# Batch 0's product from a ready-made diagonal, four turns handed to another path, and the last mix and store split by chunk

## The chip, the cores and the metric

The kernel runs on one core of a Trainium2 chip. The metric is the device time of one execution in microseconds; before the change it is 1623.7 us, the median of three executions (1623.25 to 1623.99). The profile is of one execution, with a span of 1622.2 us from its first to its last instruction.

The engines are named as in the profile: PE multiplies matrices and writes to banks of PSUM (the kernel has eight of them); PEld loads PE's weights and overlaps it; DVE and ACT work element by element; POOL does small jobs (here the power -1/2); SP issues transfers (DMA). All data here is float32, and a float32 matmul appears in the profile as two instructions, called passes here. A PE transpose is one pass pair as well: four 128x128 blocks of one batch give four instructions.

## The reference, cut to what matters

32 batches of 512 nodes with 128 features go through four graph layers that share one 512x512 adjacency matrix, each with a layer norm before it and a residual after it.

```python
# x: (32, 512, 128), adj: (512, 512)
# layer 0: normalised adjacency
h = relu(layernorm(x))
A = adj + I;  d = A.sum(-1) ** -0.5
x = x + ((d[:, None] * A * d[None, :]) @ h) @ W.T + b
# layer 1: five gated steps
h = relu(layernorm(x))
for _ in range(5):
    m = adj @ h                                   # m_in == m_out
    av = concat([m, m])
    z = sigmoid(av @ w3.T + b3 + h @ u3.T + bu3)
    r = sigmoid(av @ w4.T + b4 + h @ u3.T + bu3)
    hv = tanh(av @ w5.T + b5 + (r * h) @ u5.T + bu5)
    h = (1 - z) * h + z * hv
x = x + h
# layers 2 and 3: graph attention (2 ends in elu, 3 doesn't)
for l in (2, 3):
    h = relu(layernorm(x)) @ W_l
    e = leaky_relu((h @ a_src) + (h @ a_dst).T, 0.2)
    p = softmax(where(edge, e, -inf))
    x = x + (elu if l == 2 else identity)(p @ h)
```

## The kernel before

The kernel first records every piece of work (`op`) with its engine, an assumed cost, a due number, and what it reads and writes. When all is recorded, a list scheduler plays the program through with the assumed costs: whenever an engine is free it takes, of the pieces that are ready and find their buffers free, the one with the smallest `soon`. The order so found is the order in which the instructions are written out, so a due number is a priority on an engine and not a time. The schedule is played for some pairs (last, hurry), six times each, and the one with the earliest end is kept. `near_end` (1350) says from where on, in the scheduler's own time, a piece is ordered by how late it may be.

```python
EARLY = 8
FAR0, FAR1 = 2, 4
# ... (the scheduler)
o.soon = min(o.due, last - o.tail * hurry)                               # first try
o.soon = late[o] / self.SLOT if o.at > self.near_end else o.due          # the next ones
# ... (the buffers, then:)
    }, [(179, 0.06), (175, 0.06), (177, 0.12)], 1350, IDLE_FROM, ...)
```

Layer 0 of batches 0 to 3 multiplies by the raw adjacency plus the unit matrix. `diag` holds the four diagonal blocks with 1 added; batches 1 to 3 use it, batch 0 adds a separate multiplication by the unit matrix.

```python
diag = Val("v", C)
for m in range(C):
    op("DVE", 0.16, -6, lambda m=m: nc.vector.tensor_add(diag.t[:, m, :], block(adjT.t, m), ident.t), ...)

def product(h, due, by_diag):                    # by_diag is False for batch 0 alone
    for c in range(C):
        row = adjT.t[:, c, :]
        if by_diag:
            terms = [(0, c, row[:, :c * P]), (c, c + 1, diag.t[:, c, :]), (c + 1, C, row[:, (c + 1) * P:])]
        else:
            terms = [(0, C, row), (c, c + 1, ident.t)]
        # ... one matmul for each term that isn't empty            (L671)
    op("ACT", A, due, lambda: nc.scalar.copy(flat(m.t), flat(p.t)), ...)
```

In layer 1 a state is needed in both orientations. At its start, and after each of the five steps, it is turned either by PE (four transposes into a bank, then a copy by ACT) or by a shuttle: DVE transposes 32x32 squares, four transfers write them to DRAM and another one or four read them back in place.

```python
def to_features(y, due, *then):                  # PE's turn: 4 transposes              (L560)
def shuttle(src, squares, dst, halves, due, soon):
    # DVE transpose of squares, two halves                                             (L570)
    # 4 DMAs sq -> far (DRAM)                                                          (L577)
    # 2 DMAs far -> dst, one for each half                                             (L581)

# in ggnn(pair, due), due = 5 * pair[0]
if FAR0 <= b < B - FAR1:
    shuttle_first(h, hT, due - 2.5, due - 3)
else:
    p = to_features(h, due - 2, hT)              # and one ACT copy

# in step(b, s, m, hT, due, lane), called with due = 5 * pair[0] + 6 * s + (0 or 1)
if not EARLY <= due < STEPS * B:                 # STEPS * B = 160
    p = to_features(new, due + 2, ...)           # and two ACT copies (L796), or an addition to x after the last step
    return h, new
if not last:
    shuttle(new, None, h, True, due, due - 5)
```

The last four batches do their attention "near": no shuttle, masks in SBUF. Four chunks c of 128 nodes are mixed into two banks, two chunks in each.

```python
ps, rden, v, n = (Val("bank"), Val("bank")), Val("rden", 2), Val("v", 2), Val("r", 2)
if near:
    for j in range(C):
        def mix_from(j=j):                       # 4 chunks, 8 passes                   (L903)
            for c in range(C):
                nc.tensor.matmul(<bank c // 2, place c % 2>, e.t[:, j, c * P:(c + 1) * P], h.t[:, j, :D + 1],
                                 start=j == 0 and c % 2 == 0, stop=j == C - 1, ...)
        op("PE", C * MM1, due + 4, mix_from, r=[e[j], h[j // 2], h[2 + j // 2]], w=[*ps])
for a, p in enumerate(ps):
    op("DVE", 0.08, due + 4, <reciprocal of two chunks' sums>, ...)                  # L917
    # layer 3: two scalar_tensor_tensor, one for each chunk                           (L925)
# layer 3, near: one store for each half of the nodes, 128 KB                         (L947)
```

Of the kernel before, what the change touches and what calls it, by code (L numbers as in the profile page):

```python
# [15 lines left out]
P = 128  # L16
# [5 lines left out]
NEAR = 4  # L22
EARLY = 8
FAR0, FAR1 = 2, 4
IDLE_FROM = 1420
# [230 lines left out]
def gnn_stack(ctx: ExitStack, tc: tile.TileContext, a: dict, out: bass.AP):  # L256
# [13 lines left out]
    def flat(t):  # L270
# [33 lines left out]
        "rden": tiles(3, SMALL, "rden"),  # L304
    }, [(179, 0.06), (175, 0.06), (177, 0.12)], 1350,
        IDLE_FROM, lambda v: nc.tensor.transpose(v.t[:, 0, :], ident.t, ident.t))
# [50 lines left out]

    op("DVE", 0.2, -15, lambda: nc.vector.tensor_scalar_add(b0.t, b0.t, -1.0), w=[b0])
    for k in ("w4", "w3", "w5", "u3", "u5"):
# [5 lines left out]
    for l, w in ((2, "L2_gnn_W"), (3, "L3_gnn_w")):  # L365
        w_aug[l] = fixed([P, D + 3], f"w_aug{l}", 2)
        op("SP", 0.45, -990.5, lambda l=l, w=w: nc.sync.dma_start(w_aug[l].t[:, :D], a[w]), w=[w_aug[l][0]], delay=3.4)
        a_pair[l] = fixed([P, 2], f"a_pair{l}", 2)
        for i, k in enumerate(("src", "dst")):
            op("SP", 0.45, -990.4, lambda l=l, i=i, k=k: nc.sync.dma_start(  # L370
                a_pair[l].t[:, i:i + 1], column(a[f"L{l}_gnn_a_{k}"])), w=[a_pair[l][i]], delay=2.4)
# [18 lines left out]
    def block(t, m):  # L390
        return t[:, m, m * P:(m + 1) * P]
# [3 lines left out]
    for m in range(C):  # L395
        op("DVE", 0.16, -6, lambda m=m: nc.vector.tensor_add(diag.t[:, m, :], block(adjT.t, m), ident.t),
           r=[adjT, ident], w=[diag[m]])

    def right_factors(mT, due, passing=False):
# [13 lines left out]
        return f  # L413
    of_adj = right_factors(adjT, -5)

# [36 lines left out]

    w0T = transposed(-9.2, (one(w0), 1), then=turned)
    gates = transposed((-700, -9.5, -700, -9.5), (halves("w4"), 1), (one(raw["u3"]), 1), (halves("w3") + halves("w4", minus), 1), (halves("w5"), 1), then=turned)
    u5T = transposed(-9.4, (one(raw["u5"]), 0.5), then=turned)
    gats = transposed(-4, (one(w_aug[2]), 1), (one(w_aug[3]), 1))
    gate_b = {}
# [8 lines left out]
    for i, l in enumerate((2, 3)):  # L466
        p = Val("bank")
        op("PE", 0.3, -3, lambda i=i, l=l, p=p: nc.tensor.matmul(p.t[:, 0, :2], gats.t[:, i, :], a_pair[l].t, start=True, stop=True),
           r=[gats, a_pair[l]], w=[p])

        def columns(l=l, p=p):
            for j, (s, f) in enumerate(((1, SLOPE), (1, 1.0 - SLOPE), (0, SLOPE - 1.0))):
                nc.vector.tensor_scalar_mul(w_aug[l].t[:, D + j:D + j + 1], p.t[:, 0, s:s + 1], f)
        op("DVE", 0.3, 10, columns, r=[p], w=[w_aug[l][1]])
# [183 lines left out]

    def product(h, due, by_diag):

        p, m = Val("bank"), Val("m")
        for c in range(C):
            def times(c=c):
                row = adjT.t[:, c, :]
                if by_diag:
                    terms = [(0, c, row[:, :c * P]), (c, c + 1, diag.t[:, c, :]), (c + 1, C, row[:, (c + 1) * P:])]
                else:
                    terms = [(0, C, row), (c, c + 1, ident.t)]
                terms = [t for t in terms if t[0] < t[1]]
                for k, (lo, hi, right) in enumerate(terms):  # L670
                    nc.tensor.matmul(flat(p.t)[:, lo * P:hi * P], h.t[:, c, :], right, start=c == k == 0,  # L671
                                     stop=c == C - 1, skip_group_check=True)
            op("PE", MM if by_diag else MM + 0.1, due, times, r=[h[c], adjT, diag[c] if by_diag else ident], w=[p, m])
        op("ACT", A, due, lambda: nc.scalar.copy(flat(m.t), flat(p.t)), r=[p], w=[m])
        return m

    def normalized(begun):
# [5 lines left out]
        def turn_dinv():  # L683
            for c in range(C):
                nc.tensor.transpose(drow.t[:, c, :], dinv.t[:, c:c + 1].to_broadcast([P, P]), ident.t)
        op("PE", C * TURN, -2, turn_dinv, r=[dinv, ident, begun], w=[drow])
        op("DVE", 0.1, -790, lambda: nc.vector.tensor_mul(dinv2.t, dinv.t, dinv.t), r=[dinv], w=[dinv2])

        for m in range(C):
            op("DVE", 0.7, -1, lambda m=m: nc.vector.scalar_tensor_tensor(  # L690
                anT.t[:, m, :], adjT.t[:, m, :], dinv.t[:, m:m + 1], flat(drow.t), op0=ALU.mult, op1=ALU.mult),
# [3 lines left out]
               r=[ident, dinv2], w=[anT[m]])  # L695
        return anT, right_factors(anT, 0, True)

# [3 lines left out]
    def gcn(pair, due):  # L701
        first, ys = pair[0] < 4, []
        for i, b in enumerate(pair):
# [3 lines left out]
            else:  # L707
                norm_relu(b, y, -797 if b == 1 else due + i, dinv if first else None)
            op("DVE", V, due + i + 1, lambda b=b: nc.vector.tensor_add(
                xs[b].t, xs[b].t, b0.t[:, None, :].to_broadcast([P, C, D])), r=[b0], w=[xs[b]])  # L710
            ys.append(y)

        ms = [product(y, due + i, pair[i] > 0) for i, y in enumerate(ys)] if first else products(*ys, factors["an"], due + 1)
        if b == 1:
            factors["anT"], factors["an"] = normalized(ms[0])
        for i, (b, m) in enumerate(zip(pair, ms)):
            p = Val("bank")

            def out_mm(m=m, p=p):
                for c in range(C):  # L720
                    nc.tensor.matmul(p.t[:, c, :], m.t[:, c, :], w0T.t[:, 0, :], start=True, stop=True)  # L721
            op("PE", C * MM1, due + i + 1.5, out_mm, r=[m, w0T], w=[p])
            if first:
                for c in range(C):
                    op("DVE", 0.26, due + i + 1.5, lambda b=b, c=c, p=p: nc.vector.scalar_tensor_tensor(
                        xs[b].t[:, c, :], p.t[:, c, :], dinv.t[:, c:c + 1], xs[b].t[:, c, :], op0=ALU.mult, op1=ALU.add),
                       r=[p, dinv], w=[xs[b][c]])
# [7 lines left out]
    def ggnn(pair, due):  # L735
        hs, hTs, lanes = [], [], []
        for b in pair:
            lane, h, hT = Val("lane"), Val("h", 2), Val("hT", Q)
            op("SP", 0.0, due - 3, lambda: None, r=[xs[b]], w=[lane], delay=0)
            op("SP", 0.0, due - 3, lambda: None, r=[lane], w=[h], delay=0)  # L740
            norm_relu(b, h, due - 3)
            if FAR0 <= b < B - FAR1:
# [67 lines left out]
    def masks(begun):  # L810

        maskT = {l: fixed([P, Q, N], f"maskT{l}", C, dtype=BF16) for l in (2, 3)}
        for l in (2, 3):
            far = Val(None, C)
            far.t = tiles(1, [Q, W, C, N], f"far_mask{l}", dram, BF16)[0]
            for c in range(C):
                part = Val("mask", 1)
                edges(l, c, part, lambda part=part: part.t, 14 + l, begun)
                op("SP", 0.4, 14 + l, lambda c=c, far=far, part=part: nc.sync.dma_start(
# [11 lines left out]
    def gat(b, l, due):  # L831
# [61 lines left out]
        for j in range(C):  # L893
            op("DVE", 0.68, due + 3, lambda j=j: nc.vector.scalar_tensor_tensor(  # L894
                e.t[:, j, :], rows(row.t), h.t[:, j, D + 1:D + 2], mask(j), op0=ALU.max, op1=ALU.mult),
               r=[row, h[2 + j // 2], masked], w=[e[j]])
        ps, rden, v, n = (Val("bank"), Val("bank")), Val("rden", 2), Val("v", 2), Val("r", 2)
        if near:

            for j in range(C):  # L900
                def mix_from(j=j):
                    for c in range(C):
                        nc.tensor.matmul(flat(ps[c // 2].t).rearrange("p (c k) -> p c k", c=2)[:, c % 2, :D + 1],  # L903
                                         e.t[:, j, c * P:(c + 1) * P], h.t[:, j, :D + 1], start=j == 0 and c % 2 == 0,
                                         stop=j == C - 1, skip_group_check=True)
                op("PE", C * MM1, due + 4, mix_from, r=[e[j], h[j // 2], h[2 + j // 2]], w=[*ps])
        for a, p in enumerate(ps):
            pt = lambda p=p: flat(p.t).rearrange("p (c k) -> p c k", c=2)
            some = slice(2 * a, 2 * a + 2)
            for c in range(2 if not near else 0):  # L910
# [5 lines left out]
                op("PE", C * MM1, due + 4, mix, r=[e, h], w=[*ps] if a == c == 0 else [p])  # L916
            op("DVE", 0.08, due + 4, lambda some=some, pt=pt: nc.vector.reciprocal(rden.t[:, some], pt()[:, :, D]), r=[p], w=[rden[a]])  # L917
            if l == 2:
                op("DVE", 0.335, due + 4, lambda some=some, pt=pt: nc.vector.tensor_mul(
                    v.t[:, some], pt()[:, :, :D], rden.t[:, some, None].to_broadcast([P, 2, D])), r=[p, rden[a]], w=[v[a]])  # L920
            else:
                def finish(a=a, pt=pt):
                    for c in range(2):
                        i = 2 * a + c
                        nc.vector.scalar_tensor_tensor(xb.t[:, i, :], pt()[:, c, :D], rden.t[:, i:i + 1], xb.t[:, i, :],  # L925
                                                       op0=ALU.mult, op1=ALU.add)
                op("DVE", 2 * 0.26, due + 4, finish, r=[p, rden[a]], w=[xb[2 * a], xb[2 * a + 1]])
        if l == 2 and near:
# [16 lines left out]
        elif near:  # L945
            for a in range(2):
                op("SP", 0.45, due + 4, lambda a=a: nc.sync.dma_start(  # L947
                    out[b].rearrange("(c p) d -> p c d", p=P)[:, 2 * a:2 * a + 2], xb.t[:, 2 * a:2 * a + 2]),
                   r=[xb[2 * a], xb[2 * a + 1]])
        else:  # L950
# [3 lines left out]
    def begin(b):  # L954
        gcn((b, b + 1), STEPS * b - (16 if b == 2 else 10))

# [58 lines left out]
```

## Time and profile before

| what | value |
|---|---|
| time, median of 3 | 1623.7 us (1623.25 to 1623.99) |
| span of the profiled execution | 1622.2 us |
| DVE busy | 1378.4 us (85% of the span) |
| ACT busy | 725.3 us (45%) |
| DMA queue of the kernel's transfers | 39.0% of 16 engines' span |
| PE's first instruction | 1.05 us after the start |
| PE's turns (L560): of new states, of first states, of the attention's input | 48, 24 and 32 instructions, four to a turn |

Busy time is the union of the durations that the profile gives. For PE those durations overlap: an instruction is shown from its start to a modelled end, while the next one starts earlier than that. What a group of PE's instructions takes from the next group is therefore read from the distance between starts, or from the chain of work, which merges neighbours and counts no time twice. The chain of work is followed back from the last instruction: at each step to whatever released it, or else to the instruction before it on the same engine.

### The profile page before, as it was taken

What the parts mean: (1) busy time and instruction counts of PE and PEld (TensorE: products, weight loads), DVE (VectorE), ACT (ScalarE), POOL (GpSimd) and SP (SyncE); (2) the same over time, 40 slices, a digit from 0 to 9 for tenths busy, and PEclk for the clock granted to TensorE, in tenths of its full rate; (3) what the DMA queues carried; (4) which work ended last, traced back from release to release, by engine and by line L of the source; (5) the groups of instructions that cost most, each with busy time, mean ns of one, the idle gap of its engine ahead of it and who ended that gap; (6) DMA issues with size and microseconds to landing.
All of it is one profiled execution on the core that took longest, in us unless ns stands there. A gap on an engine that the chain in (4) does not pass through costs nothing.

```text
span 1622.2 us, 24004 instructions
## 1 busy us (share of the span) xinstructions
PE 1614.2 (100%) x7326; PEld 1168.2 (72%) x7326; DVE 1378.4 (85%) x3971; ACT 725.3 (45%) x1628; POOL 146.4 (9%) x137
## 2 busy tenths in 40 slices
PE   9999999999999999999999999999999999999998
PEld 8666667776776777777777776777767686677778
DVE  8968588888888898888898888988888788888888
ACT  5644453535345353453544345343453524443554
POOL 2200000011001110001010011000010000000100
PEclk9999999999999999999999999999999999999999
DMA  4134243544535344353543535345353343334101
GB/s 131 27 78 117 66 115 87 131 100 102 124 79 138 92 105 115 90 132 78 129 106 92 137 79 123 99 100 128 85 128 87 85 99 78 104 97 112 40 22 52
DMA packets 374177, 157.72 MB, mean 97 GB/s; under 512 B 201664, under 2 KB 355616, under 8 KB 374048
## 3 DMA queue, kind: packets, MB, share of 16 engines
q1 hardware_dynamic: 373760, 155.67, 39.0%
q8 instruction: 58, 0.95, 0.2%
q14 instruction: 71, 0.58, 0.1%
q10 hardware_dynamic: 288, 0.52, 0.1%
HBM read 86.25 MB, written 69.84 MB: 96 GB/s over the span
## 4 chain that ended last, share of the span: by engine, by line
PE 94%; DVE 3%; DMA 1%; ACT 0%; POOL 0%; issue 0%; SPq 0%; DVEq 0%; ACTq 0%; POOLq 0%
PE bank L628 33%; PE bank L914 12%; PE bank L762 8%; PE bank L763 8%; PE bank L776 8%; PE bank L769 8%; PE bank L777 8%; PE bank L852 3%; PE bank L721 2%; PE bank L903 2%; PE bank L671 1%; PE bank L560 1%; DVE st L480 0%; POOL rstd L493 0%; DMA e<-in_adj_dram 0%
## 5 line engine op out<-in xcount | busy, mean ns | idle before, releaser
L493 POOL TENSOR_TENSOR rstd<-ve,mhalf 128x4 f32<-128x4 f32 x119 | 135.1, 1137 | 1382.2 <-DVE ve L485 1243.4
L628 PE MATMUL bank<-made,S 128*128 128x256 f32 x960 | 230.7, 380 | 0.5 <-DVE m L641 0.3
L914 PEld LDWEIGHTS bank<-h_gat,e 128*128 128x128 f32 x1792 | 210.6, 191 | 13.0 <-issue 10.5
L633 ACT COPY half<-bank 128x256 f32<-128x256 f32 x282 | 104.6, 371 | 243.6 <-PE bank L628 239.1
L914 PE MATMUL bank<-h_gat,e 128*128 128x129 f32 x1792 | 212.4, 275 | 0.0
L628 PEld LDWEIGHTS bank<-made,S 128*128 128x128 f32 x960 | 184.2, 196 | 31.3 <-issue 12.3
L765 ACT ACTIVATE r<-bank,gate_bw 128x512 f32<-128x512 f32 x160 | 109.6, 685 | 206.3 <-PE bank L763 188.9
L781 DVE TENSOR_TENSOR hv<-hv,hT 128x512 f32<-128x512 f32 x160 | 109.2, 683 | 81.7 <-ACT hv L779 81.5
L767 DVE SCALAR_TENSOR_TENSOR rh<-r,hT 128x512 f32<-128x512 f32 x160 | 109.7, 686 | 67.6 <-ACT r L765 65.8
L762 PE MATMUL bank<-m,wT 128*128 128x512 f32 x320 | 163.6, 593 | 0.1
L776 PE MATMUL bank<-m,wT 128*128 128x512 f32 x320 | 163.5, 592 | 0.0
L763 PE MATMUL bank<-hT,wT 128*128 128x512 f32 x320 | 163.4, 592 | 0.0
L777 PE MATMUL bank<-rh,wT 128*128 128x512 f32 x320 | 163.4, 592 | 0.0
L779 ACT ACTIVATE hv<-bank,gate_bw 128x512 f32<-128x512 f32 x160 | 109.7, 686 | 119.5 <-PE bank L777 119.4
L769 PE MATMUL bank<-m,wT 128*128 128x512 f32 x320 | 163.1, 592 | 0.0
L894 DVE SCALAR_TENSOR_TENSOR e<-row,h_gat,maskT 128x512 f32<-128x512 f32 x224 | 160.7, 741 | 0.0
L628 PE MATMUL bank<-adjT,h 128*128 128x256 f32 x640 | 159.7, 380 | 0.0
L628 PEld LDWEIGHTS bank<-adjT,h 128*128 128x128 f32 x640 | 123.0, 196 | 25.9 <-issue 14.4
L641 DVE TENSOR_TENSOR m<-half,bank 128x256 f32<-128x256 f32 x282 | 115.8, 413 | 26.9 <-PE bank L628 15.7
L771 ACT ACTIVATE z<-bank,gate_bw 128x512 f32<-128x512 f32 x160 | 109.5, 685 | 42.6 <-PE bank L769 39.9
L480 DVE BATCH_NORM_STATS2 st<-x 128x6 f32<-128x128 f32 x480 | 116.0, 279 | 7.0 <-DMA x<-in_x_dram 6.7
L763 PEld LDWEIGHTS bank<-hT,wT 128*128 128x128 f32 x320 | 60.8, 190 | 76.5 <-issue 76.1
(146 smaller groups left out, 2366.9 us busy)
## 6 DMA issues: line engine op xcount, KB each, us to landing
far<-sq SPq DMA_DIRECT2D x920, 64.0 KB
h<-far SPq DMA_DIRECT2D x240, 128.0 KB
gT<-far SPq DMA_DIRECT2D x56, 256.0 KB
row<-line SPq DMA_DIRECT2D x56, 256.0 KB
x<-in_x_dram SPq DMA_DIRECT2D x32, 256.0 KB
h<-far SPq DMA_DIRECT2D x28, 256.0 KB
out_dram<-x SPq DMA_DIRECT2D x28, 256.0 KB
hT<-far SPq DMA_DIRECT2D x104, 64.0 KB
```

The source lines that it names most:

```text
L480: op("DVE", 0.21, due, lambda c=c: nc.vector.bn_stats(st.t[:, c, :], xb.t[:, c, :]), r=[xb[c]], w=[st[c]])
L493: op("POOL", 1.0, due, lambda: nc.gpsimd.tensor_tensor(rstd.t, ve.t, mhalf.t, ALU.pow), r=[ve, mhalf], w=[rstd])
L628: nc.tensor.matmul(low(r), u[:, l, :], factors[k][0]()[:, l, :], start=fresh and l == 0, stop=l == 1, skip_group_check=not fresh)
L641: op("DVE", HV, due - 5, lambda: nc.vector.tensor_add(out(), u.t, low(t)), r=[u, t], w=[o])
L762: nc.tensor.matmul(flat(gate.t), gates.t[:, 0, :], flat(m.t), start=True, stop=False)
L763: nc.tensor.matmul(flat(gate.t), gates.t[:, 1, :], flat(hT.t), start=False, stop=True)
L767: op("DVE", V, due - 5, lambda: nc.vector.scalar_tensor_tensor(flat(rh.t), flat(r.t), 1.0, flat(hT.t), op0=ALU.add, op1=ALU.mult), r=[r, h ...
L769: op("PE", MM, due + 0.3, lambda: nc.tensor.matmul(flat(gate.t), gates.t[:, 2, :], flat(m.t), start=False, stop=True, skip_group_check=Tru ...
L776: nc.tensor.matmul(flat(cand.t), gates.t[:, 3, :], flat(m.t), start=True, stop=False)
L777: nc.tensor.matmul(flat(cand.t), u5T.t[:, 0, :], flat(rh.t), start=False, stop=True)
L894: op("DVE", 0.68, due + 3, lambda j=j: nc.vector.scalar_tensor_tensor(e.t[:, j, :], rows(row.t), h.t[:, j, D + 1:D + 2], mask(j), op0=ALU. ...
L914: nc.tensor.matmul(pt()[:, c, :D + 1], e.t[:, j, i * P:(i + 1) * P], h.t[:, j, :D + 1], start=(j == 0), stop=(j == C - 1))
```

## The change

It has five parts.

1. Batch 0 uses the diagonal tile as batches 1 to 3 do. The multiplication by the unit matrix goes; the four additions that make the tile come earlier in DVE's order.
2. `EARLY` goes from 8 to 6. The states of batches 0 and 1 after the second step (s = 1, due 6 and 7) are shuttled instead of turned by PE.
3. `FAR1` goes from 4 to 2. The first states of batches 28 and 29 are shuttled as well.
4. For batch 31's layer 3, the mix goes into four banks, one for each chunk. Its last two sources are taken chunk by chunk, and each chunk is divided, added and stored by itself (64 KB).
5. Many due numbers of the first slots and the scheduler's pairs of (last, hurry) and `near_end` are set anew.

```diff
-EARLY = 8
-FAR0, FAR1 = 2, 4
+EARLY = 6
+FAR0, FAR1 = 2, 2
-    }, [(179, 0.06), (175, 0.06), (177, 0.12)], 1350,
+    }, [(167, 0.1), (181, 0.05)], 1300,
-    op("DVE", 0.2, -15, ... b0.t, b0.t, -1.0 ...)
+    op("DVE", 0.2, -38.7, ...)
-        op("SP", 0.45, -990.5, ... w_aug ..., delay=3.4)
+        op("SP", 0.45, -990.5, ... w_aug ..., delay=5)
-        op("DVE", 0.16, -6, ... diag ...)
+        op("DVE", 0.26, -800 + 0.7 * m, ... diag ...)
-    of_adj = right_factors(adjT, -5)
+    of_adj = right_factors(adjT, -3.6)
-    w0T = transposed(-9.2, ...)
-    gates = transposed((-700, -9.5, -700, -9.5), ...)
-    u5T = transposed(-9.4, ...)
-    gats = transposed(-4, ...)
+    w0T = transposed(-11.7, ...)
+    gates = transposed((-700, -9.5, -700, -15.8), ...)
+    u5T = transposed(-15.2, ...)
+    gats = transposed(-0.4, ...)
-        op("PE", 0.3, -3, ... a_pair ...)
+        op("PE", 0.3, 9, ... a_pair ...)
-    def product(h, due, by_diag):
+    def product(h, due):
-                if by_diag:
-                    terms = [(0, c, row[:, :c * P]), (c, c + 1, diag.t[:, c, :]), (c + 1, C, row[:, (c + 1) * P:])]
-                else:
-                    terms = [(0, C, row), (c, c + 1, ident.t)]
+                terms = [(0, c, row[:, :c * P]), (c, c + 1, diag.t[:, c, :]), (c + 1, C, row[:, (c + 1) * P:])]
-        op("PE", C * TURN, -2, turn_dinv, ...)
+        op("PE", C * TURN, -6.4, turn_dinv, ...)
-            op("DVE", 0.7, -1, ... anT ...)
+            op("DVE", 0.7, 3.2, ... anT ...)
-        return anT, right_factors(anT, 0, True)
+        return anT, right_factors(anT, -16.5, True)
-            op("DVE", V, due + i + 1, ... x + b0 ...)
+            op("DVE", V, due + i + 3.8, ...)
-            op("PE", C * MM1, due + i + 1.5, out_mm, ...)
+            op("PE", C * MM1, due + i + 3.3, out_mm, ...)
-                    op("DVE", 0.26, due + i + 1.5, ... x of layer 0 ...)
+                    op("DVE", 0.26, due + i - 0.5, ...)
-            norm_relu(b, h, due - 3)
+            norm_relu(b, h, due - 2)
-                edges(l, c, part, lambda part=part: part.t, 14 + l, begun)
+                edges(l, c, part, lambda part=part: part.t, -2.7 + l, begun)
-        gcn((b, b + 1), STEPS * b - (16 if b == 2 else 10))
+        gcn((b, b + 1), STEPS * b - (13.8 if b == 2 else 10))

-        ps, rden, v, n = (Val("bank"), Val("bank")), Val("rden", 2), Val("v", 2), Val("r", 2)
+        apart = near and l == 3 and b == B - 1
+        per = 1 if apart else 2
+        ps, rden, v, n = [Val("bank") for _ in range(C // per)], Val("rden", C), Val("v", 2), Val("r", 2)
-            for j in range(C):
-                op("PE", C * MM1, due + 4, mix_from, r=[...], w=[*ps])
+            for js, cs in [([j], range(C)) for j in range(2 if apart else C)] + [((2, 3), [c]) for c in range(C if apart else 0)]:
+                op("PE", len(js) * len(cs) * MM1, due + 4, lambda js=js, cs=cs: mix_from(js, cs),
+                   r=[...], w=[*ps] if len(js) == 1 else [ps[cs[0]]])
     # reciprocal, multiply-add: for `per` chunks at a time instead of two
-            for a in range(2):
-                op("SP", 0.45, due + 4, ... out[...][:, 2 * a:2 * a + 2], xb.t[:, 2 * a:2 * a + 2] ...)
+            for a in range(0, C, per):
+                op("SP", 0.45, due + 4, ... out[...][:, a:a + per], xb.t[:, a:a + per] ...)
     # ... (cut: the same expressions with `per` and `chunks`)
```

## The prediction

> **What bounds the kernel now.** I read the page first, for the share of each engine and the chain that ended last.
>
> ```profile
> PE 1614.2 (100%) x7326; PEld 1168.2 (72%) x7326; DVE 1378.4 (85%) x3971; ACT 725.3 (45%) x1628; POOL 146.4 (9%) x137
> ...
> PE 94%; DVE 3%; DMA 1%; ACT 0%; POOL 0%; issue 0%; SPq 0%; DVEq 0%; ACTq 0%; POOLq 0%
> ```
>
> PE is busy all the time and is 94% of the chain. A busy PE may still hide gaps, because its ends are modelled, so I asked for PE's waits, which is the second view (line, releaser: us in total, times, longest).
>
> ```profile
> PE bank L340 <- DVE hv L333: 1.1, 1, 1.1
> PE bank L628 <- ACT half L633: 0.9, 2, 0.5
> PE bank L628 <- DVE m L641: 0.6, 2, 0.3
> PE bank L903 <- DVE e L894: 0.5, 1, 0.5
> PE bank L383 <- DMA e<-in_adj_dram: 0.4, 1, 0.4
> PE bank L628 <- DVE S L616: 0.2, 1, 0.2
> ```
>
> That is 3.7 us of waits in 1622. To be sure, I summed PE's passes by the distance of their starts in the timeline: 0.429 us for 512 columns, 0.324 for 384, 0.216 for 256, 0.112 for 128 to 131. With the counts of the groups this is 1608 x 0.429 + 12 x 0.324 + 2644 x 0.216 + 3062 x 0.112 = 1608 us. The first pass starts at 1.05 us, and 4.05 us lie behind the last one. 1608 + 1 + 4 = 1613, so at most 9 to 10 us of the span is neither work nor the two ends. Of those some 4 lie in the first 50 us (the 16 run-up passes take 0.21 each at the start instead of 0.11, which is 1.7; adjacency not there yet, 0.7; the rest small), 1 in the last 20, and 4 to 5 between. No passes inserted only to keep PE going (their line is absent from the groups) are there to absorb a saving. So the kernel gets faster by the PE work that goes, by a shorter end, and hardly by anything else.
>
> **What the Trainium skill says.** "Perfetto Trace Analysis", section "Tensor Engine Instruction (MATMUL, LD_WEIGHTS)": the shown end of a PE instruction is estimated from its size. The trace agrees: 512-column passes are shown with 592 ns and start 430 ns apart. Hence the sums above use starts. "TensorE: Matmul & The Clock Gate", section "Back-to-back issue gap": the distance is the columns over the clock and a constant of about 2.5 ns. The page's numbers are for shorter types, but the form holds in this trace: four times the columns, 0.429 against 0.112, so cutting a row of 512 into three pieces costs nearly nothing, and dropping 128 columns saves 0.11 per pass. The same page, "Part 4: PE-mode transpose": a turn ends in PSUM and needs a copy out; here the two copies of a state take 0.69 us of ACT. "DMA: Bandwidth & Descriptors", section "Rules for kernel authors": under 64 KB a transfer is mostly overhead. The end of this trace is in keeping: the last store of 128 KB lands 2.4 us after its issue, so I expect little from halving it.
>
> **The change part by part.**
>
> *Batch 0's product.* The chain of work in order of time (start, us, what) shows batch 0 with the unit matrix (16 passes) and batch 1 with the tile (20):
>
> ```profile
> 9.46 4.33 PE bank L671 x16
> 13.79 1.12 PE bank L438 x10
> 14.91 3.49 PE bank L671 x20
> ```
>
> The difference is 4.33 - 3.49 = 0.84 us. It agrees with the work: 4 chunks x 2 passes x 128 columns = 8 x 0.109 = 0.87. I take -0.84. The tile's four additions (0.28 us each, about 1 us in all) exist already, at 8.0 to 11.5 us; they now stand ahead of batch 1's statistics. Batch 1's first input came at 12.8 us and PE used it at 14.64, so that second of delay is covered, though PE is done with batch 0 earlier by as much. Net cost: 0 to 0.3.
>
> *PE's turns.*
>
> ```profile
> L560 PE MATMUL bank<-ident,hT 128*128 128x128 f32 x48 | 7.2, 273 | 0.0
> L560 PE MATMUL bank<-ident,h 128*128 128x128 f32 x24 | 3.6, 284 | 0.0
> ```
>
> 48 instructions are 12 turns of states: 4 of batches 0 and 1 (s = 0 and 1) and 8 at the end with due 160 or more. 24 are 6 turns of first states: batches 0, 1 and 28 to 31. `EARLY` = 6 takes the two of s = 1, `FAR1` = 2 those of 28 and 29. The chain gives 0.44 for each turn, so PE loses 4 x 0.44 = 1.75 us of work. ACT loses 2 x 0.69 + 2 x 0.59; DVE gains 4 x 0.77 = 3.1 us of square transposes.
>
> *Latency of the new shuttles.* A comparable shuttle in the timeline, that of a state of batches 2 and 3:
>
> ```profile
> 79.32 0.77 DVE L570 STREAM_TRANSPOSE sq<-hT 128x256 f32<-128x256 f32 x2
> ...
> 80.12 1.78 SPq L577 DMA_DIRECT2D far<-sq  x4
> 83.32 1.30 SPq L581 DMA_DIRECT2D h<-far  x2
> ```
>
> From the finished state (79.3) to the second hop's last issue (84.6) are 5.3 us, and with 2.4 us to landing, as for the last store, 7.7. PE's turn needs 0.44 and 0.69. The turns that go stand at 73.8 and 76.8, and the next product of that pair starts at 84.1. With shuttles its inputs are there at about 81.1 and 84.1, and four DVE sums follow. So it is late by 0 to 1.5 us, while the products and output of batches 6 and 7 are at hand. DVE is about 78% busy from 70 to 85 us and has room. For 28 and 29 the pipeline is full; nothing is to be lost there. Cost: +0.3, up to 1.5.
>
> *The end.*
>
> ```profile
> 1612.77 5.38 PE bank L903 x48
> 1618.15 0.02 issue
> 1618.17 0.17 DVE rden L917
> 1618.34 0.25 DVE x L925
> 1618.59 0.26 DVEq L1011
> 1618.85 0.52 DVE x L925 x2
> ```
>
> PE is done at 1618.15. DVE then has two chunks' sums and four multiply-adds to go, to 1619.37; the last store's issue begins at 1619.39 and lands at 1622.2. Split, PE finishes a chunk every 4 x 0.112 = 0.45 us; for the last one DVE needs only 0.17 + 0.33, so its store could start 0.5 us after PE's end instead of 1.24. But the issues in the trace stand 0.52 apart, which is more than 0.45: four of them, the first 0.84 before PE's end, put the fourth at 0.7. Gain 1.24 - 0.7 = 0.5, and a little for half the bytes (estimate 0.2): -0.7. PE's work is the same, 32 passes. Taking the last two sources together can make PE wait for the fourth row of `e`, but that row was done at 1615.6 and would be needed at 1616.4.
>
> *Due numbers.* They move no work between engines, only order. What they can win is some of the 4.7 us of gaps after the first 50 us, and what they can lose is as open. As they were evidently set to suit the other parts, I put -0.9.
>
> Sum: -0.84 - 1.75 - 0.7 + 0.1 + 0.3 - 0.9 = -3.8, from 1623.7 to 1619.9.
>
> **The rivals.**
>
> *DVE takes over the beginning.* The chain from 28 to 50 us is DVE's: 4.8 to 5.0 busy of each 5 us. The change adds DVE work nearby and moves the normalised adjacency later (from -1 to 3.2). Against it: PE waits only 0.2 us in that stretch, and the added squares come 25 us later. If it came true, PE would starve for some us: 1622 to 1625.
>
> *The shuttles' latency replaces the turns.* If no other pair has work at 78 to 86 us, the 0.87 saved on batches 0 and 1 turns into a wait of 1 to 2. For it: only three pairs are under way then. Against: the scheduler counts 4 and 5 us for the two hops, and had a pair's layer 0 at hand. Time then 1621 to 1622.
>
> *The new order has other gaps.* All the order changes, and a scheduler with assumed costs is wrong somewhere; the old order shows gaps of 0.2 to 0.6 at 49, 104, 106, 173, 325, 357 and 397 us. A worse draw gives 3 to 4 back (1623 to 1624), a better one takes 3 more (1617).
>
> **Range and chances.** The work and the end, about -3.3, I hold for nearly sure. What is left is the order's gaps, whose total is 5.7 us after the first 50 us: they can hardly fall by more than 3, and I see no source for more than 3 new ones. Time 1619.9, range 1617.4 to 1622.6. Two per cent are 32 us, ten times the sum, so within 2% is almost certain: 0.985; faster 0.005, slower 0.01.
>
> **What would show it.** After: no L671 passes with the unit matrix, and batch 0's product as long as the others' (3.5 us). PE's turns: 40 and 16 instructions instead of 48 and 24, and PE's number of passes down by 12: minus 16 for the turns, plus 4 for batch 0 (8 unit passes gone, 12 added by the cuts). From PE's end to the span's end 3.3 us instead of 4.05, with four stores 0.5 apart. PE's waits between 3 and 6 us. I am wrong if PE's waits rise above 7 us, which means that the order or the shuttles cost more than the work saved, or if the time falls below 1617, which means that gaps I took for fixed (the first 50 us above all) could be closed.

## The result and the profile after

The changed kernel takes 1618.09 us (median of 6, 1618.00 to 1618.34), the kernel before beside it 1623.54 (1623.10 to 1623.99): 5.45 us less, a ratio of 0.9967 with a 95% interval of 0.9954 to 0.9979. The span of the profiled execution fell from 1622.2 to 1616.2.

The page of the changed kernel, the busy time of each engine and the chain by engine:

```profile
PE 1609.5 (100%) x7314; PEld 1166.0 (72%) x7314; DVE 1379.3 (85%) x3981; ACT 723.0 (45%) x1622; POOL 143.1 (9%) x137
...
PE 96%; DVE 2%; DMA 1%; ACT 0%; issue 0%; SPq 0%; DVEq 0%; ACTq 0%
```

PE has 12 passes fewer, as foretold. Its turns in the groups of instructions (out<-in, shape, count, busy us and mean ns, idle before):

```profile
L560 PE MATMUL bank<-ident,hT 128*128 128x128 f32 x40 | 5.8, 273 | 0.0
L560 PE MATMUL bank<-ident,h 128*128 128x128 f32 x16 | 2.5, 281 | 0.0
```

40 and 16 in place of 48 and 24: four turns are gone. PE's waits in the changed kernel (line, releaser: us in total, times, longest):

```profile
PE bank L340 <- DVE hv L333: 1.1, 1, 1.1
PE bank L628 <- ACT half L633: 0.5, 1, 0.5
PE bank L383 <- DMA e<-in_adj_dram: 0.4, 1, 0.4
```

The two of the first microseconds (L340, L383) remain. Behind them there were 2.2 us of waits, and there are 0.5.

Waits shorter than the modelled ends don't appear in that view. So I split the span as in the prediction: the distance from each PE start to the next, less the usual distance for that shape, is a gap. The table sums gaps by stretch ("9-50" is from 9 to 50 us of the span), in us; keep-going passes (inserted by the scheduler where it foresees idle time) count as gaps at 0.11 each. The first column of gaps includes PE's slow passes at the start. "End" is the time after the last pass has been issued. A row's work, gaps and end, with the 1.05 us ahead of the first pass, add up to its span.

| kernel | keep-going passes | work | 0-9 | 9-50 | 50-450 | 450-1350 | 1350 on | end | span |
|---|---|---|---|---|---|---|---|---|---|
| before | 0 | 1607.2 | 3.4 | 0.7 | 3.4 | 0.7 | 1.6 | 4.2 | 1622.2 |
| after | 0 | 1604.6 | 2.8 | 0.4 | 0.5 | 0.5 | 2.0 | 4.4 | 1616.2 |
| difference | 0 | -2.6 | -0.6 | -0.2 | -3.0 | -0.2 | +0.4 | +0.2 | -6.0 |

The work fell as predicted. The end did not get shorter. And the gaps fell by 3.6 us, most of it between 50 and 450 us. In these 400 us lie all five waits of L628 in the prediction's view (L628 is the product that two batches share); in the changed kernel that stretch has none. The busy time by stretch shows that without any model of mine (columns: stretch, its length, then busy us and instructions of PE, PEld, DVE, ACT, POOL, granted clock, DMA share, GB/s). Before:

```profile
50.00:150.00 100.00, 99.29 (x355) 66.08 (x356) 76.41 (x223) 47.79 (x100) 9.75 (x8) 1.00 0.31 72
150.00:250.00 100.00, 99.54 (x361) 66.09 (x360) 76.18 (x202) 44.32 (x91) 6.43 (x6) 1.00 0.42 97
250.00:350.00 100.00, 99.88 (x471) 73.81 (x470) 88.40 (x255) 42.17 (x95) 9.78 (x8) 1.00 0.44 106
350.00:450.00 100.00, 99.60 (x448) 71.51 (x447) 85.88 (x244) 42.93 (x98) 8.07 (x8) 1.00 0.45 106
```

After:

```profile
50.00:150.00 100.00, 100.00 (x375) 69.74 (x374) 78.77 (x253) 48.96 (x105) 11.83 (x11) 1.00 0.29 63
150.00:250.00 100.00, 99.90 (x358) 64.34 (x357) 77.55 (x193) 43.41 (x83) 4.06 (x4) 1.00 0.50 117
250.00:350.00 100.00, 100.00 (x450) 72.43 (x449) 85.24 (x231) 42.87 (x94) 6.36 (x6) 1.00 0.43 105
350.00:450.00 100.00, 100.00 (x451) 72.44 (x450) 87.14 (x257) 45.33 (x102) 9.64 (x9) 1.00 0.42 105
```

PE idles 1.69 us in these 400 us before and 0.10 after; the rest of the 3.0 hides under modelled ends. So the experiments had three questions: what closed the gaps, why the end stayed as long as it was, and whether the work is worth what it was said to be.

### The profile page after: what moved, and what is told of

Its sections match the earlier page's. It is cut to its first block, busy times and chain, and to the rows that moved or that the text cites. A ratio compares the mean times of both kernels' runs of the same rounds, so it can differ in the third digit from the quotient of the medians.

```text
span 1616.2 us, 24006 instructions
## 1 busy us (share of the span) xinstructions
PE 1609.5 (100%) x7314; PEld 1166.0 (72%) x7314; DVE 1379.3 (85%) x3981; ACT 723.0 (45%) x1622; POOL 143.1 (9%) x137
## 4 chain that ended last, share of the span: by engine, by line
PE 96%; DVE 2%; DMA 1%; ACT 0%; issue 0%; SPq 0%; DVEq 0%; ACTq 0%
PE bank L628 35%; PE bank L917 12%; PE bank L759 8%; PE bank L760 8%; PE bank L774 8%; PE bank L766 8%; PE bank L773 8%; PE bank L849 3%; PE bank L718 2%; PE bank L668 1%; PE bank L903 1%; DVE e L891 1%; PE bank L560 1%; DMA e<-in_adj_dram 0%; DMA maskT<-far_mask 0%
## 5 line engine op out<-in xcount | busy, mean ns | idle before, releaser
L493 POOL TENSOR_TENSOR rstd<-ve,mhalf 128x4 f32<-128x4 f32 x119 | 131.8, 1108 | 1375.9 <-DVE ve L485 1054.9
L628 PE MATMUL bank<-made,S 128*128 128x256 f32 x960 | 231.4, 380 | 0.1
L628 PEld LDWEIGHTS bank<-made,S 128*128 128x128 f32 x960 | 184.1, 196 | 31.4 <-issue 12.0
L628 PE MATMUL bank<-adjT,h 128*128 128x256 f32 x640 | 158.5, 379 | 0.0
L628 PEld LDWEIGHTS bank<-adjT,h 128*128 128x128 f32 x640 | 123.4, 196 | 26.7 <-issue 15.1
```

The source lines that it names most:

```text
L493: op("POOL", 1.0, due, lambda: nc.gpsimd.tensor_tensor(rstd.t, ve.t, mhalf.t, ALU.pow), r=[ve, mhalf], w=[rstd])
L628: nc.tensor.matmul(low(r), u[:, l, :], factors[k][0]()[:, l, :], start=fresh and l == 0, stop=l == 1, skip_group_check=not fresh)
```

## The experiments

Each kernel ran beside the kernel before on the same chip. That one's median was 1623.53 in the first group (`a_` and `u_`), 1623.34 in the second (`f_` and `n_`) and 1622.94 in the third (`r_` and `m_`), so differences are given against the one of the same group.

### One half of the change at a time

`a_orders` is the kernel before with the due numbers and the pairs of the changed kernel. `a_parts` is the opposite: all the rest of the change, under the old due numbers and pairs.

```diff
 # a_orders, against the kernel before
-    }, [(179, 0.06), (175, 0.06), (177, 0.12)], 1350,
+    }, [(167, 0.1), (181, 0.05)], 1300,
+    # and all due numbers of the change; diag for batch 0, EARLY, FAR1, apart as before
```

> The kernel before with only the due numbers and the scheduler's pairs set anew; product, turns and end as before. Theory 1 (the new order closes PE's gaps): the 3.5 us that the change took from the gaps are all here, 1623.5 - 3.5 = 1620.0, between 1619.3 and 1620.8, and PE's waits in the page fall below 2.5 us. Theory 2 (the gaps closed because PE has fewer turns and a shorter first product, the order being what fits that): 1622.8 to 1624. Theory 3 (every new order draws its gaps anew, by chance): anything from 1618.5 to 1625.

> The changed kernel with the old due numbers and the old pairs: new product, fewer turns, split end. Theory 1: only the work goes, 2.6 us, 1623.5 - 2.6 = 1620.9, between 1620.2 and 1621.6, and the gaps from 50 to 400 us stay. Theory 2: 1618.0 to 1619.0, as the changed kernel. Theory 3: anything from 1617 to 1624.

`a_orders`: 1625.15, 1.6 us slower than before (ratio 1.0011, 1.0005 to 1.0018). `a_parts`: 1626.17, 2.6 slower (1.0014, 1.0008 to 1.0021), although 2.6 us of PE's work are gone. Each half of a change that wins 5.45 us loses by itself. Theories 1 and 2 fall, and both times lie even above the widest range given, that of theory 3; what is left is theory 3, or something that ties the halves together.

Two more kernels divide the orders themselves: `u_dues` is the changed kernel with the old due numbers, `u_ends` the changed kernel with the old pairs and `near_end`.

```diff
 # u_ends, against the changed kernel
-    }, [(167, 0.1), (181, 0.05)], 1300,
+    }, [(179, 0.06), (175, 0.06), (177, 0.12)], 1350,
```

> The changed kernel with the old due numbers but the new pairs. If the due numbers close the gaps (theory 1): as a_parts, 1620.2 to 1621.6. If the pairs do it: 1618.0 to 1618.8. Theory 3: far from both.

> The changed kernel with the old pairs and near_end but the new due numbers. If the due numbers close the gaps: within 0.6 of the changed kernel, 1617.5 to 1618.7, with differences in the last 250 us alone. If the pairs do it: 1620 or more. Theory 3: far from both.

`u_dues`: 1622.10, 1.4 less than before (0.9991, 0.9983 to 1.0000), which fits none of its ranges. `u_ends`: 1623.12, not to be told from before (0.9997, 0.9989 to 1.0005), so the pairs and `near_end` together are worth about 5 us to the changed kernel. The same split by stretch:

| kernel | keep-going passes | 9-50 | 50-450 | 450-1350 | 1350 on |
|---|---|---|---|---|---|
| a_orders | 8 | 0.7 | 1.6 | 0.8 | 4.1 |
| a_parts | 11 | 2.3 | 1.5 | 0.0 | 7.4 |
| u_dues | 8 | 2.2 | 1.7 | 0.3 | 3.2 |
| u_ends | 19 | 1.0 | 0.2 | 0.5 | 7.4 |

The pairs and `near_end` show in the last stretch: where they were chosen for another version, there are 3 to 7 us of gaps instead of 2, and keep-going passes, which neither the kernel before nor the changed one has. The due numbers show in the first 450 us.

### How fine the choice of the order is

`n_near` moves `near_end` of the changed kernel from 1300 to 1310, and nothing else.

> The changed kernel with near_end 1310 instead of 1300: nothing but the order from about 1190 us on changes, by a hair's breadth of the scheduler. Theory 1 (due numbers and pairs are good by what they mean): within 0.6 of 1618.1. Theory 3 (each order draws its gaps, and the changed kernel holds a good draw): slower by 1 to 5 us, 1619 to 1623, with waits and keep-going passes in the last 250 us.

1623.97 (1.0004, 0.9995 to 1.0012): the whole gain is gone. The keep-going passes in its groups of instructions:

```profile
L306 PE MATMUL bank<-ident 128*128 128x128 f32 x20 | 3.2, 273 | 0.0
```

PE's instructions are the same as the changed kernel's for the first 1226 us, and then another order follows, with 7.1 us of gaps from 1350 us on instead of 2.0. Theory 3 is right in this: a setting that differs by a hair makes an order that is 6 us longer on the chip. But the chip is not what draws here. The scheduler runs before any instruction is written, so the end that it sees for its order is known without the chip: 1614.95 us for the changed kernel, and 1620.84 for `n_near`, 5.9 more.

### Each half with a pair of its own

If a pair and a `near_end` fit only the version they were sought for, the halves were compared unfairly above. For the next kernels I let the kernel's own scheduler play 224 pairs with each of four values of `near_end` (1250, 1300, 1360, 1430), and took the one whose end it sees earliest.

```diff
 # r_orders is a_orders, r_parts is a_parts, r_tail the changed kernel with apart = False; each with its pair:
+    }, [(175, 0.12)], 1360,     # r_orders
+    }, [(175, 0.04)], 1360,     # r_parts
+    }, [(176, 0.06)], 1250,     # r_tail
```

> As a_orders (only the due numbers new), but with a pair and a near_end sought for it: the one of 224 pairs and four values of near_end for which the scheduler of this version sees the earliest end. Theory 4 (a pair fits only the version for which it was sought, and a_orders was slow because its pair was the other version's): no keep-going passes, 1621 to 1622.5, that is 1.5 to 2 faster than the kernel before by the gaps from 50 to 400 us. Theory 5 (the new due numbers do harm without the other parts): 1624 or more again.

> As a_parts (new product, fewer turns, split end, old due numbers), with a pair sought for it in the same way. Theory 4: no keep-going passes, the 2.6 us of work gone and the gaps as in the kernel before: 1620 to 1621.5. Theory 5 (the parts do harm under the old due numbers): 1624 or more again.

`r_orders`: 1622.43, 0.5 less than before, which is not to be told from nothing (0.9999, 0.9991 to 1.0007); against the kernel before of its group it is 2.1 better than `a_orders`, but the 1.5 to 2 us expected from the gaps did not come. `r_parts`: 1620.30, 2.6 less than before (0.9984, 0.9978 to 0.9991), and in the same way 5.3 better than `a_parts`. Neither has keep-going passes. So theory 4 holds: what made the halves slow was the pair with its `near_end`. With their own, the parts are worth as much as the PE work that they save, 2.6 us, and the due numbers alone next to nothing.

The end that each version's scheduler sees for its order had said most of this (us, both columns less those of the kernel before, whose scheduler sees 1619.17):

| kernel | scheduler's end | measured time |
|---|---|---|
| a_parts | +5.0 | +2.6 |
| n_near | +1.7 | +0.6 |
| u_dues | +1.1 | -1.4 |
| u_ends | +0.5 | -0.4 |
| a_orders | +0.5 | +1.6 |
| r_orders | -1.5 | -0.5 |
| r_parts | -1.9 | -2.6 |
| changed kernel | -4.2 | -5.45 |
| r_tail | -4.8 | -5.7 |
| m_best | -4.9 | -5.6 |

(The last two follow below.) The scheduler is off by up to 2.5 us, but it sees the three fastest orders as the three fastest.

The two halves together are worth 5.45, and that is 2.3 more than the sum of the two. Most of the surplus lies at the start. The timeline of `a_parts`, PE first and then ACT (start, us, line, what, idle before and its releaser); `r_parts` has the same order there:

```profile
14.26 0.82 PE L438 MATMUL bank<-ident,w_aug 128*128 128x128 f32 x4 [0.62 <-DMA w_aug<-in_L_gnn_W_dram]
14.92 0.39 PE L668 MATMUL bank<-v,y 128*128 128x128 f32 x2
```

```profile
13.04 1.65 ACT L499 ACTIVATE y<-x,off,rstd 128x128 f32<-128x128 f32 x4
```

Batch 0's product is over at 12.4, and batch 1's first chunk is ready at about 13.4. But the turns of `w_aug`, attention weights that are needed much later, stand ahead of batch 1 in PE's order, and their load comes at 14.2. In the kernel before these turns came at 27.9. The new due numbers repair this: `u_dues`, which lacks them, has the same wait (0.49 us), and the changed kernel hasn't. That it is these of them is likely but was not tried one by one: the load's assumed delay goes from 3.4 to 5, the turns' due number from -4 to -0.4, and the other weights go into the middle of batch 0's product. The changed kernel's chain of work in order of time (start, us, what):

```profile
8.82 0.91 PE bank L668 x4
9.73 0.89 PE bank L438 x8
10.62 2.62 PE bank L668 x16
13.25 0.22 PE bank L438 x2
13.47 3.56 PE bank L668 x20
```

Batch 1 follows at 13.47 without a wait. From 9 to 50 us `r_parts` has 2.3 us of gaps (1.0 of them at these turns), the kernel before 0.7, the changed kernel 0.4: the due numbers take back what the parts lose there.

The gaps from 50 to 450 us are no part of the surplus: 3.4 before, 1.6 and 1.4 in `r_orders` and `r_parts`, 0.5 with both, so each half alone closes more than half of them. Up to some 1220 us all versions with the same parts and due numbers have one and the same PE order, whatever their pair. These are therefore four orders and no more, and why the fourth has the fewest gaps is not shown.

### Batch 0's product by itself

`f_unit` keeps every piece of work of the changed kernel in its place and only writes batch 0's product with full rows and the unit matrix again.

```diff
 for c in range(C):
     ...
+    if unit:                       # batch 0 alone; cost, due number and inputs of the piece as before
+        terms = [(0, C, row), (c, c + 1, ident.t)]
```

> The changed kernel, scheduled as it is, but batch 0's product is written out with the full rows and the unit matrix again, so that no instruction of any engine changes its place. If the term is what the chain of work showed: 0.84 us more than the changed kernel, 1618.1 + 0.8 = 1618.9, between 1618.6 and 1619.3. If PE would only wait for batch 1's statistics in the time it saved: 1618.0 to 1618.3.

1619.15 (0.9972, 0.9962 to 0.9983). The two kernels of the same group that share its order, `f_store2` and `f_queues`, take 1618.22 and 1618.24: 0.9 us, as the term of 0.84 said. The pieces of the product in its chain of work:

```profile
8.73 1.20 PE bank L670 x4
9.93 0.89 PE bank L438 x8
10.82 3.25 PE bank L670 x12
```

They add up to 4.45 us, against 0.91 + 2.62 = 3.53 in the changed kernel: 0.92 more. (`f_store2` ran at two levels, see the last section; against its lower executions, near 1618.1, it is 1.1.)

### The end

In the timeline of the changed kernel's last microseconds SP has six stores in a row (SPq: the issue of transfers; DVE L920 is the reciprocal, L927 the multiply-add):

```profile
1609.80 2.17 PE L903 MATMUL bank<-h_gat,e 128*128 128x129 f32 x18
...
1610.74 2.87 SPq L949 DMA_DIRECT2D out_dram<-x  x6
...
1612.09 0.59 DVE L927 SCALAR_TENSOR_TENSOR x<-bank,rden,x 128x128 f32<-128x128 f32 x2
```

PE is done at 1611.97, the last chunk at 1612.68, but the last issue ends at 1613.61: two of the six belong to batch 30 and stand right ahead. Two kernels take this apart, both with every piece in the changed kernel's place: `f_store2` stores batch 31 as two transfers again, `f_queues` has ACT issue two of the four.

```diff
 # f_queues
-                op("SP", 0.45, due + 4, lambda a=a: nc.sync.dma_start(...))
+                q = nc.scalar if a % 2 else nc.sync
+                op("SP", 0.45, due + 4, lambda a=a, q=q: q.dma_start(...))
```

> The changed kernel, scheduled as it is, with four banks and chunk by chunk up to the store, but batch 31 is stored as two transfers of 128 KB instead of four of 64 KB. Theory A (the end is bound by SP's issues, six of them 0.5 us apart): the last issue starts right after the last chunk, 0.5 us earlier, and a transfer of twice the size lands some 0.25 later: 0.2 to 0.4 less than the changed kernel, 1617.8. Theory B (the size of the last transfer sets the end): 0.2 to 0.5 more, 1618.5.

> The changed kernel, scheduled as it is, but the stores of chunks 1 and 3 of batch 31 are issued by ACT instead of SP. Theory A (SP's issues bind): the fourth store starts 0.55 us earlier, 1618.1 - 0.5 = 1617.6, between 1617.4 and 1617.9. Theory B (size or the fixed end): 1618.0 to 1618.3.

1618.22 (0.9972, 0.9961 to 0.9982) and 1618.24 (0.9966, 0.9953 to 0.9979): by the time, neither differs from the changed kernel, and theory A's gains are not there. In the trace of `f_queues` theory A is half right:

```profile
1612.59 1.09 ACTq L950 DMA_DIRECT2D out_dram<-x  x2
1612.70 0.59 DVE L927 SCALAR_TENSOR_TENSOR x<-bank,rden,x 128x128 f32<-128x128 f32 x2
```

The last issue now ends at 1613.68, 0.39 after the last chunk (1613.29) instead of 0.93. From PE's last pass to the end of the span it is 3.9 us instead of 4.3. But that execution lost 0.8 us more in its first 9 us, where the adjacency came later, and so the span is no shorter; the times don't settle 0.4 us.

So SP's queue is one half of the matter. The other is what follows the last store. In `r_parts` batch 30's stores are issued earlier. The last of the six below, which takes 0.37 us, starts 0.71 us after PE's end (1615.09), just as predicted. And yet the span ends 4.13 after it:

```profile
1613.24 2.94 SPq L949 DMA_DIRECT2D out_dram<-x  x6
```

The last bytes are on their way at 1620.8 in the kernel before, at 1614.4 in the changed one and at 1617.0 in `r_parts`, and nothing of the stores follows, but these moments are 1.3, 1.8 and 2.2 us ahead of the span's end (1622.2, 1616.2 and 1619.2). In this order, with the columns of the busy times above:

```profile
1620.80:1620.90 0.10, 0.00 (x0) 0.00 (x0) 0.00 (x0) 0.00 (x0) 0.00 (x0) 1.00 0.10 21
1614.40:1614.50 0.10, 0.00 (x0) 0.00 (x0) 0.00 (x0) 0.00 (x0) 0.00 (x0) 1.00 0.07 16
1616.95:1617.05 0.10, 0.00 (x0) 0.00 (x0) 0.00 (x0) 0.00 (x0) 0.00 (x0) 1.00 0.10 21
```

The same from the traces of six kernels (us after PE's end; "closing" is from the end of the last store's last packet to the end of the span):

| kernel | batch 31's stores | last issue starts | last packet ends | closing | span ends |
|---|---|---|---|---|---|
| before | 2 | 1.26 | 2.73 | 1.31 | 4.05 |
| r_tail (below) | 2 | 1.26 | 2.73 | 1.76 | 4.50 |
| f_store2 | 2, four banks | 0.74 | 2.20 | 1.89 | 4.09 |
| changed kernel | 4 | 1.28 | 2.48 | 1.78 | 4.26 |
| f_queues | 4, two queues | 0.74 | 1.96 | 1.92 | 3.88 |
| r_parts | 4 | 0.71 | 1.93 | 2.19 | 4.13 |

A store of 64 KB is through 1.2 us after its issue, one of 128 KB 1.47. So the split does bring the last bytes forward, by 0.25 us in the changed kernel and by 0.8 in `r_parts`. But the closing, in which the engines pass semaphores and drain, is longer than in the kernel before, by 0.45 to 0.9 us. The split is not the cause, since `r_tail` has it too. A load of 8 KB of instructions goes with it: in the 14 traces the three closings without one last 1.30 to 1.31 us, the eleven with one 1.46 to 2.19. Whether it is the cause was not tried.

`r_tail`, the changed kernel without the split and with a pair of its own, asks for the worth of the split as a whole:

> The changed kernel without the split of the last mix and store, with a pair sought for it. If the split brings what the prediction gave it: 0.7 us more than the changed kernel, 1618.8. If it brings nothing (six stores one behind the other in SP's queue): within 0.4 of the changed kernel, 1617.7 to 1618.5.

1617.25 (0.9968, 0.9955 to 0.9980), 5.7 less than the kernel before beside it, where the changed kernel was 5.45 less. No worth of the split is to be seen in the time. Its order of the last quarter is another one, though (1.2 us of gaps from 1350 us on instead of 2.0), so a few tenths are not excluded.

### A version that might beat both

`m_best` has both of these: two queues for the last stores, and a pair sought for it, (180, 0.14) with `near_end` 1250.

> The changed kernel with a pair sought in the same way, and with the stores of chunks 1 and 3 issued by ACT. Theory 4: the changed kernel's own pair is already near the best, and this one is within 1 us of it, 1617.0 to 1618.3; in the trace the end lies 3.9 us behind PE's last pass, as with the two queues before, instead of 4.3.

1617.32 (1617.07 to 1617.46; 0.9964, 0.9951 to 0.9978), 5.6 less than before. That is lower than the changed kernel's 1618.09, but the kernel before was 0.6 lower in that group too. I don't call it faster. Its end lies 3.8 us behind PE's last pass, where 3.9 was expected. What it shows is that the changed kernel's own pairs were already about as good as the one of some 900 whose end the scheduler sees earliest.

## Why the prediction was right, and where it was not

The time lies within the range, at its lower end. By the steps:

- *What bounds the kernel*: right. 2.6 us of PE's work less made `r_parts` 2.6 us faster. DVE's busy time hardly changed (1378.4 and 1379.3); the 3.1 us of transposes expected to be added don't show in it.
- *Batch 0's product*, -0.84: right, 0.9 by `f_unit`. That batch 1's delay is covered was right too: its first chunk is ready just when PE comes to it. Not foreseen was that with the new product and the old due numbers turns whose load is late stand there, which costs `a_parts` 0.8 us and is gone with the new due numbers.
- *PE's turns*, -1.75: right in count (four turns, 12 passes fewer in all), and with the product the 2.6 us that `r_parts` shows. The turns alone were not isolated: to undo them changes the whole order.
- *Latency of the new shuttles*, +0.3: no cost is seen. PE is busy for 100.00 of the 100 us from 50 to 150. The 2.4 us to landing in that sum are too long, as the next point says.
- *The end*, -0.7: wrong; the span's end came 4.26 us after PE's instead of 3.3. The prediction reads the last store as landing at 1622.2, 2.4 us after its issue. That is the end of the span: the last packet ended at 1620.87, 1.47 after the issue began, and 1.31 us of closing followed, which it took as part of the store. Two of its terms were right, half the bytes (0.26 us, estimate 0.2) and, where the queue was free (`r_parts`), the fourth issue (0.71, forecast 0.7). What failed is the queue in the changed kernel, where batch 30's two stores push the last issue to 1.28, and the closing, which grew from 1.31 to 1.78.
- *Due numbers*, -0.9: that the order can close gaps was right, and the guess that the due numbers were set to suit the other parts fits what `r_orders` and `r_parts` show; the size was wrong. After the first 9 us the gaps fell by 3.0 us. The bound held: after 50 us they fell from 5.7 to 3.0, by no more than 3. What did not hold is that no source of more than 3 new ones was seen: `a_parts`, `u_ends` and `n_near` have over 5 us more than before after 1350 us alone. PE's waits, forecast at 3 to 6 us, are 2.0.
- Of the rivals, the third came closest: the new order has fewer gaps, near the better draw that it names (1617), and neighbours of it (`n_near`, `u_ends`) have 5 to 6 us more.

From 9 us on the profiles give -2.6 of work, -3.0 of gaps and +0.2 at the end, -5.4 in all, near the measured 5.45; the other 0.6 between the two spans lie in the first 9 us, where the last section says what varies. So the -3.8 became -5.45 by two errors of opposite sign: the order's terms (-0.9 and +0.4 for delays) came out at -3.0, and the end's -0.7 at +0.2. The order's share of the gain was luck as far as the prediction goes: nothing in it could tell this order from that of `n_near`, whose time of 1623.97 lies outside the range. The scheduler's own ends, 1619.17 and 1614.95, could have told it.

## What to carry to other kernels

Where one engine is busy throughout and an order made by a scheduler feeds it, each change has two effects: the work that it removes, which can be counted beforehand, and a new order, which here was worth from -3 us to +5. The order's part is not blind chance: the end that the scheduler sees can be read before anything runs, and here it named the fastest orders. Compare versions only after each has had its order sought anew, or freeze the order and change only what a piece writes out. Before splitting a last store, look at what stands ahead of it in the same queue, and at what of the time behind it is the store at all.

## What was not expected of the hardware

PE's first transposes run at either of two speeds. In the changed kernel's profile and in that of `f_store2` (timeline of PE, as above):

```profile
5.66 1.82 PE L383 MATMUL bank<-ident,e 128*128 128x128 f32 x12 [0.43 <-DMA e<-in_adj_dram]
```

```profile
6.56 2.82 PE L383 MATMUL bank<-ident,e 128*128 128x128 f32 x12 [0.51 <-DMA e<-in_adj_dram]
```

Twelve passes took 1.82 us in one and 2.82 in the other, with starts 0.21 apart, as in the run-up. The granted clock is shown as 1.00 for both, but that is no measurement: the traces' record of the clock begins only at 4.62 us in the changed kernel and at 10.46 in `f_store2`, and a view shows 1.00 where there is no record. Over the 14 traces the record begins anywhere from 4.62 to 10.46 us, and in each the first passes stand 0.21 apart ahead of it and 0.11 behind it. That is what varies in the first 9 us: in the profile of the kernel before it begins at 7.22.

The five lower executions of `f_store2` took 1617.94 to 1618.33, the three others, the profiled one among them, 1620.18 to 1620.65. Of the 2.2 us by which the span of the profiled one exceeds the changed kernel's, 1.8 lie in the first 9 us; the other two were not traced. The Trainium skill's page "TensorE: Matmul & The Clock Gate", section "What's actually happening", says that the clock starts at half and is released by about 3.4 us of activity, counted in windows that run freely. The trace agrees: the two speeds are a factor of two apart, and the stretches of full clock in the 14 records last 1607.68, 1611.09, 1614.50 or 1617.92 us, in steps of 3.41.
